# A four-layer conditioned transformer on one core: values by twos, layer 3's activations, negated minima, tables on GpSimd, lent score banks

## The chip, the core and the metric

The kernel runs on one core of a Trainium2 chip. Five engines work beside each other, each through a queue of its own in program order: TensorE (PE in the profile, its weight loads PEld), VectorE (DVE), ScalarE (ACT), GpSimd (POOL) and SyncE (SP), which issues most of the transfers. The metric is the time of one execution on the device in microseconds; less is better.

## The reference

Four layers follow each other on x of shape (4, 512, 512). All arithmetic is in float32. Every layer is conditioned on a vector of 512 per batch element. Cut to what matters:

```python
def layer0(x, t_emb, ...):            # 16 query heads of 32, 4 key heads, a window of 64 and every 64th token
    h = layernorm(x) * (1 + scale) + shift
    q = rope(h @ Wq.T); c = h @ Wkd.T; k = rope(c @ Wku.T); v = c @ Wvu.T
    attn = softmax(where(mask, -inf, q @ k.T / sqrt(32)))
    return x + (attn @ v) @ Wo.T

def layer1(x, pos, t, ...):           # 8 query heads of 64, 1 key head; then a gated MLP of 2048
    h = rms(x) * (w1 * (1 + t @ tw1.T))
    q = rope(h @ Wq.T, pos); k = rope(h @ Wk.T, pos); v = h @ Wv.T
    x = x + (softmax(q @ k.T / 8) @ v) @ Wo.T
    h = rms(x) * (w2 * (1 + t @ tw2.T))
    return x + (silu(h @ Wg.T) * (h @ Wu.T)) @ Wd.T

def layer2(x, cond, bias, ...):       # 16 heads of 32, normalised q and k; then an MLP of 2048
    h = ln(x) * (scale1 + 1) + shift1
    q, k, v = h @ Wqkv.T + [q_bias, 0, v_bias]
    q = q / max(norm(q), 1e-12) * sm; k = k / max(norm(k), 1e-12)
    x = x + (softmax(q @ k.T + bias) @ v @ Wproj.T + bproj) * gamma1
    h = gelu_tanh((ln(x) * (scale2 + 1) + shift2) @ Wfc1.T + bfc1)
    return x + (h @ Wfc2.T + bfc2) * gamma2

def layer3(x, emb, ...):              # 8 experts on 64 channels each, 64 -> 256 -> 64
    h = gelu(einsum('btel,elf->btef', x, W1) + b1)
    y = einsum('btef,efl->btel', h, W2) + b2
    hn = layernorm(y, g, b) * (1 + scale) + shift
    return x + silu(hn) @ out_W + out_b
```

## The kernel before

Tokens stand on the 128 partitions in four tiles of 128 (NT = 4), channels in four chunks of 128 (NC = 4). A weight unit of 512x512 (1 MB) is loaded as one transfer; rings of such units are loaded ahead.

Two streams run beside each other on TensorE and are woven by a planner. Stream A does the attention of layers 0 and 1 (stage a01) and of layer 2 (a2) for one batch element, stream M the MLPs: layer 1's (m1), layer 2's with layer 3 (m2). At the start there is no MLP yet, so M does batch 0's a01 while A does batch 1's. At the end A does batch 3's layer 2 MLP and the second half of its tokens in layer 3 (half1), M the first half (half0). A third strand, `conditioning`, computes the scales and shifts of all layers from ten weight units that pass one buffer (`late`) in turn.

Each stage is a Python generator that records operations and yields what it waits for. `Clocks` keeps a planned time for each engine and tile, with costs for each operation (`length`, `matmul`); `interleave` takes the next step from the stream whose inputs are ready and that is furthest behind its place. `evict` copies a bank from PSUM on ACT or DVE, whichever the plan has free sooner. At the end all operations are emitted in the order of their planned starts, so each engine's order is fixed in the built program. Because the calls go through one recorder, most rows of the profile have one line: L301 for DVE, ACT and POOL, L354 for matrix products, L360 for transposes, and the rows are told apart by their tiles.

PSUM has three pools of two: `two` (psS), tiles of two banks that take scores, and the banks of side A (psA) and side M (psM). `Side.bank` hands out a bank of its own side, `Side.at` says when one is free. Tile names: two = scores; probs and wm = probabilities of side A and M; pT and hid = transposed probabilities of side A and M (hid also hidden units); t and mt = work tiles; nq and mn = normed tokens or turned queries; h and mT = turned activations; late = the conditioning's unit, layer 1's table scratch, and later the bias of layer 2.

One attention unit is four heads (or two pairs) of one tile of 128 queries. `scores` makes products into two `two` tiles, takes the row maximum (`maxima`, or a plain reduction in layer 1), negates it in an own small operation (tile neg), and `soften` does the exponential with a sum on ACT, the reciprocal on DVE and the normalisation on POOL. `back` turns the probabilities by transposes through a side bank, and `values` multiplies them with v. `attention` runs them as a pipeline: the scores of unit i+1 go ahead of unit i's turning, and values follow two units behind, one unit at a time: a group of products into one bank and one eviction of 128 queries per unit.

Layer 2's attention first makes q, k, v by token tile: four tiles of q2, four of k2 (`product`), then four of v2; each q or k tile is copied by DVE, squared on ACT, reduced on DVE, raised to -1/2 on POOL (tile inv), multiplied on POOL, and turned (`heads_T`) one product later.

Layer 3 (`experts`): `first` takes for a pair of experts and each half f two banks, adds the bias to one on DVE and to the other on ACT, and then takes the Gelu over the whole hid tile in place; `second` and `third` make and turn y. Then `norm` (statistics on whole rows of 512, `norm_steps`), `turned` with gain and lift, a Silu over all four chunks, and the output's products.

Layer 1's rope tables (`tables`, `trig`: sine and cosine with an exact reduction of the angle) are computed on DVE for all positions at once (128x512), when batch 0's attention of layer 0 is about to begin; the conditioning waits for them, as they use its buffer.

Of the kernel before, what the change touches and what calls it, by code (L numbers as in the profile page):

```python
# [12 lines left out]
F32 = mybir.dt.float32  # L13
# [11 lines left out]
LOWEST = -3.0e38  # L25
# [283 lines left out]
def cond_seq_kernel(ctx: ExitStack, tc: tile.TileContext, a: dict, out: bass.AP):  # L309
# [89 lines left out]

    class Side:  # L400
# [8 lines left out]
        def bank(self):  # L409
            return clocks.tile(self.row_tag + "bank", 2, self.pools[0], (P, 512), "bank", name("bank"))  # L410

        def at(self, k=1):

            return clocks.free(self.row_tag + "bank", 2, k)
# [12 lines left out]
    class AttentionSide(Side):  # L427
# [28 lines left out]
        def pair(self):  # L456
            t = two_banks()
            return [t[:, 0, :], t[:, 1, :]]

        def pair_at(self):  # L460
            return clocks.free("two", 2)

    class OtherSide(Side):
# [25 lines left out]

        def pair(self):  # L490
            return [self.bank(), self.bank()]

        def pair_at(self):
            return self.at(2)
# [72 lines left out]
    def trig(ang, k, e, sin, nsin, cos):  # L567


        r = ang  # L570

        def nearest(period):
            vector.tensor_scalar(k, r, 1.0 / period, MAGIC, ALU.mult, ALU.add)
            vector.tensor_scalar(k, k, -MAGIC, None, ALU.add)

        def less(part):
            vector.scalar_tensor_tensor(r, k, -part, r, ALU.mult, ALU.add)

        far = TWO_PI * 2.0**17
        big = split(far, 2.0**8, 12, 2)  # L580
        nearest(far)
        less(big[0])
        less(big[1])
        vector.tensor_scalar(e, k, big[2], None, ALU.mult)
        nearest(TWO_PI)
        for part in split(TWO_PI, 2.0**-4, 7, 4):
            less(part)
        vector.tensor_tensor(r, r, e, ALU.subtract)
        nearest(TWO_PI)
        for part in split(TWO_PI, 2.0**-9, 12, 2):  # L590
            less(part)
        vector.tensor_scalar(r, r, PI_F32, -PI_F32, ALU.min, ALU.max)
        scalar.activation(e, r, AF.Abs)
        scalar.activation(sin, r, AF.Sin)
        scalar.activation(cos, e, AF.Sin, bias=half_pi, scale=-1.0)
        vector.tensor_scalar(nsin, sin, -1.0, None, ALU.mult)

    def tables(label, n, half, tokens, freqs):
# [3 lines left out]
        vector.tensor_tensor(  # L602
# [5 lines left out]
        parts = [const.tile([P, n * half], F32, name=f"{label}_{i}") for i in range(3)]  # L608
        trig(ang, k, e, *parts)
        return [t.rearrange("p (t i) -> p t i", i=half) for t in parts]  # L610
# [31 lines left out]
    def norm_steps(n, src, eps, rms=False, tiles=range(NT)):  # L642

        mv, own = tiny([P, NT, 2], "mv"), slice(tiles[0], tiles[-1] + 1)
        for t in tiles:
            st = tiny([P, 6], "st")
            vector.bn_stats(st, src[:, t, :])
# [83 lines left out]
    def maxima(p, s, bias, width, scale):  # L731

        mx = tiny([P, 2], "mx")
        for j in range(2):
            vector.tensor_tensor_reduce(
                out=p[:, j, 0:width], in0=s[:, j, 0:width], in1=bias, scale=scale, scalar=LOWEST,
                op0=ALU.add, op1=ALU.max, accum_out=mx[:, j : j + 1],
            )
        neg = tiny([P, 2], "neg")
        vector.tensor_scalar(neg, mx, -1.0, None, ALU.mult)  # L740
# [4 lines left out]
    def attention(side, units, scores, back, values, work, first, final=True):  # L745
# [15 lines left out]

        yield Until(scorable, of=first)
# [3 lines left out]
        for i, u in enumerate(units):  # L766
            cost, more = 0.0, i + 1 < len(units)
            when = [scorable] if more else []
            if len(late) == 2:
                yield Until(*when, side.at, of=late[0][1])  # L770
                values(*late.pop(0))
                cost += work[1]
            else:
                yield Until(*when)
# [9 lines left out]
        for u, pT in late:  # L784
            yield Until(side.at, of=pT)
            values(u, pT)
            yield work[1]
# [81 lines left out]
    coefs, tabs, ended = {}, {}, set()  # L869
# [16 lines left out]
    def attention0(b, side):  # L886
# [4 lines left out]
        if "0" not in tabs:  # L891
            tabs["0"] = tables("tab0", NT, 16, tok, freq[:, 32:48])
# [61 lines left out]
        def scores(u):  # L954
# [11 lines left out]
            for q, sc in zip(p, s):  # L966
                neg = maxima(q, sc, bias, n, 1.0 / math.sqrt(32.0))
                soften(q, q, neg, n, 1.0)
# [19 lines left out]
        def values(u, pT):  # L988
            c, qt = u
            (pT,), o, bl = pT, side.bank(), blocks(qt)  # L990
            for i, (at, n) in enumerate(bl):
                for g in range(4):
                    mm(
                        o[quarter(g), 0:P], lhsT=v[0:n, qt, i, quarter(g)],
                        rhs=pT[0:n, i, g * P : (g + 1) * P], start=i == 0, stop=i == len(bl) - 1,
                    )
            evict(ctxT[:, c, qt * P : (qt + 1) * P], o[:, 0:P])

        if "1" not in tabs:

            posf = const.tile([P, B * NT], F32, name="posf")
            vector.tensor_copy(posf, pos_i)
            tabs["1"] = tables("tab1", B * NT, 32, posf, freq[:, 0:32])
            ringC.load(1)
# [6 lines left out]
    def attention1(b, side):  # L1011
        n, wkv1 = side.n(), (yield from unit_for(b, "wkv1"))
        norm(n, xs[b], 1e-6, rms=True)
        yield from known("n1")
        hT = side.h()
# [66 lines left out]
        def values(u, pT):  # L1082
            c2, qt = u
            o = side.bank().rearrange("p (i q) -> p i q", q=P)
            for i in range(2):
                for at in range(NT):
                    for j in range(2):
                        mm(
                            o[half(j), i, :], lhsT=v[:, at, :], rhs=pT[i][:, j, at, :],
# [599 lines left out]
```

## Time and profile before

| | |
|---|---|
| median of 3 runs | 2498.31 us (2492.44 to 2498.45) |
| the profiled execution | 2497.25 us |
| its span, first to last instruction | 2495.5 us |
| mean granted TensorE clock | 0.992 |
| transposes of probs, 128x128 | 1600, 228.8 us busy |
| ACT table loads | 39, 50.0 us |
| DMA read | 147.83 MB, 61 GB/s with what is written |

A row of a group reads: line, engine, operation, out<-in, sizes, count | busy us and mean ns of one | the engine's idle time just before them and what ended most of it. A product in float32 leaves two records on TensorE, a transpose one. In a timeline the columns are start, length, engine, line, operation; the bracket is the engine's idle time before it and its releaser. Records of TensorE overlap, so the time that one takes from the engine is read from start to start.

### The profile page before, as it was taken

The numbers are of one execution on the slowest core, as the hardware profiler recorded it, in microseconds if no ns is written. First come the engines' busy times: TensorE is split into PE (matmuls) and PEld (weight loads), VectorE is DVE, ScalarE is ACT, GpSimd is POOL, SyncE is SP. The second block draws the span as 40 slices with busy tenths as digits, with TensorE's granted clock in tenths as the row PEclk, the third lists the DMA queues.
The fourth block names the chain that finished last, engine by engine and source line by source line (L and its number), as shares of the span: only waits on it lengthen the run. The fifth ranks groups of instructions, "written<-read, shape, count | busy, mean of one in ns | idle before, by whom it ended". The sixth has DMA issues, their size and how long they took to land.

```text
span 2495.5 us, 33420 instructions
## 1 busy us (share of the span) xinstructions
PE 2432.5 (97%) x12564; PEld 1242.0 (50%) x12564; DVE 1190.5 (48%) x3180; ACT 877.6 (35%) x2071; POOL 733.5 (29%) x921
## 2 busy tenths in 40 slices
PE   7989999999999999999999999999999999999997
PEld 4555655444554555554455455554455444554443
DVE  6766552133654454625554455443465333763233
ACT  2645441002551351414353043333255202651233
POOL 2433320005332223324222232424332205533221
PEclk9999999999999999999999999999999999999998
DMA  3220122220113111111211111112111221102210
GB/s 112 100 74 18 52 68 68 86 87 34 35 52 106 51 52 55 39 68 55 89 48 61 63 69 65 42 56 72 68 35 52 83 89 53 44 32 95 72 55 21
DMA packets 83312, 154.18 MB, mean 62 GB/s; under 512 B 3584, under 2 KB 10784, under 8 KB 83152
## 3 DMA queue, kind: packets, MB, share of 16 engines
q1 hardware_dynamic: 82544, 151.83, 17.9%
q8 instruction: 100, 1.64, 0.3%
q14 instruction: 60, 0.49, 0.1%
q0 software_dynamic: 176, 0.15, 0.1%
q10 hardware_dynamic: 432, 0.07, 0.0%
HBM read 147.83 MB, written 4.21 MB: 61 GB/s over the span
## 4 chain that ended last, share of the span: by engine, by line
PE 88%; DVE 3%; issue 3%; ACT 2%; POOL 2%; DMA 1%; ACTq 0%; POOLq 0%; DVEq 0%
PE bank L354 71%; PE bank L360 11%; PE two L354 6%; POOL inv L301 1%; ACT probs L301 1%; DVE probs L301 1%; ACT wm L301 0%; DVE neg L301 0%; POOL t L301 0%; DVE pT L301 0%; DMA late_ada_g<-in_units 0%; DMA wm<-in_units 0%; DVE t L301 0%; DMA late_ada_t<-in_units 0%; POOL probs L301 0%
## 5 line engine op out<-in xcount | busy, mean ns | idle before, releaser
L301 POOL TENSOR_SCALAR probs<-probs,inv 128x512 f32<-128x512 f32 (+4 forms) x544 | 316.4, 596 | 688.4 <-DVE inv L301 579.4
L301 ACT ACTIVATE probs<-probs,neg 128x512 f32<-128x512 f32 (+2 forms) x448 | 265.4, 594 | 254.8 <-DVE neg L301 254.3
L360 PEld LDWEIGHTS bank<-ident,probs 128*128 128x128 f32 (+2 forms) x1744 | 201.9, 141 | 161.9 <-issue 128.6
L360 PE MATMUL bank<-ident,probs 128*128 128x128 f32 (+2 forms) x1744 | 245.4, 276 | 4.1 <-ACT arow L301 1.2
L354 PE MATMUL bank<-mT,wm_gate 128*128 128x512 f32 x512 | 248.9, 597 | 0.0
L354 PE MATMUL bank<-mT,wm_up 128*128 128x512 f32 x512 | 245.7, 597 | 0.0
L354 PE MATMUL bank<-wm_down,hid 128*128 128x512 f32 x512 | 239.6, 596 | 0.7 <-DVE hid L301 0.7
L301 DVE CUSTOM_DVE_ANT_0 probs<-two,late 128x512 f32<-128x512 f32 x256 | 166.2, 686 | 74.3 <-PE two L354 56.4
L354 PE MATMUL bank<-wm_fc,hid 128*128 128x512 f32 x384 | 187.6, 594 | 0.0
L354 PE MATMUL bank<-mT,wm_fc 128*128 128x512 f32 x384 | 182.6, 597 | 0.0
L301 ACT COPY pT<-bank 128x512 f32<-128x512 f32 (+2 forms) x240 | 133.8, 580 | 83.8 <-PE bank L360 75.8
L354 PEld LDWEIGHTS bank<-pT,v 128*32 128x32 f32 (+2 forms) x3488 | 110.7, 116 | 95.9 <-issue 33.3
L354 PE MATMUL bank<-pT,v 128*32 128x128 f32 (+2 forms) x3488 | 146.0, 278 | 8.3 <-DVE pT L301 5.8
L301 ACT ACTIVATE mt<-bank 128x512 f32<-128x512 f32 x64 | 37.8, 591 | 327.6 <-PE bank L354 327.6
L354 PE MATMUL bank<-wa_q,h 128*128 128x512 f32 x320 | 152.4, 599 | 0.2 <-DVE t L301 0.2
L301 DVE TENSOR_TENSOR x<-x,bank 128x512 f32<-128x512 f32 x100 | 68.4, 684 | 176.1 <-PE bank L354 176.0
L354 PE MATMUL two<-kT,nq 32*128 32x512 f32 (+5 forms) x1088 | 150.0, 539 | 1.1 <-DVE mx L301 1.1
L354 PEld LDWEIGHTS bank<-wm_down,hid 128*128 128x128 f32 x512 | 91.7, 190 | 98.1 <-issue 96.2
L354 PEld LDWEIGHTS bank<-mT,wm_up 128*128 128x128 f32 x512 | 91.0, 190 | 98.2 <-issue 97.7
L301 DVE RECIPROCAL inv<-total 128x2 f32<-128x2 f32 x320 | 53.0, 166 | 172.9 <-ACT probs L301 155.7
L354 PEld LDWEIGHTS bank<-mT,wm_gate 128*128 128x128 f32 x512 | 90.0, 190 | 90.8 <-issue 90.3
L301 DVE COPY pT<-bank 128x512 f32<-128x512 f32 (+2 forms) x199 | 131.1, 680 | 5.9 <-PE bank L360 5.0
(221 smaller groups left out, 3396.3 us busy)
## 6 DMA issues: line engine op xcount, KB each, us to landing
wm_fc<-in_units SPq DMA_DIRECT2D x24, 1024.0 KB, 5.6
wm_gate<-in_units SPq DMA_DIRECT2D x16, 1024.0 KB, 5.7
wm_up<-in_units SPq DMA_DIRECT2D x16, 1024.0 KB, 5.7
wm_down<-in_units SPq DMA_DIRECT2D x16, 1024.0 KB, 5.4
wa_q<-in_units SPq DMA_DIRECT2D x10, 1024.0 KB, 5.5
wa_fc<-in_units SPq DMA_DIRECT2D x8, 1024.0 KB, 5.5
wa_o<-in_units SPq DMA_DIRECT2D x6, 1024.0 KB, 5.7
wa_k<-in_units SPq DMA_DIRECT2D x4, 1024.0 KB, 5.6
```

The source lines that it names most:

```text
L301: return call(*map(real, args), **{k: real(x) for k, x in kw.items()})
L354: latest[0] = nc.tensor.matmul(real(out), lhsT=real(lhsT), rhs=real(rhs), **kw)
L360: latest[0] = nc.tensor.transpose(real(out), real(src), unit)
```

## The change

The values of two units are taken together: `attention` waits until both are turned, and `values` gets both, fills one bank with 256 queries and evicts once. `maxima` becomes `lowest`: scores are scaled by the negative factor and the minimum is taken, which is the negated maximum, so the small negation goes; the exponential's scale is -1. (Layer 1's own reduction keeps its negation.) The mask or bias is added to the negated scores as it is.

Layer 1's tables are made by a generator of single operations on GpSimd, which `interleave` steps beside the streams (`chores`); a fused multiply-add becomes a multiply and an add there. Attention of layer 1 and the conditioning wait for them by name.

A `two` tile may be lent as a bank while no attention is between its first scores and its last values (`scoring`).

In layer 2 the products are ordered q2 x 4, k2 0, k2 1, then v2 0, k2 2, v2 1, k2 3, v2 2, v2 3; k is copied by `evict`, and the multiply with the inverse norm is on DVE.

In layer 3 the first products of a pair fill two `two` tiles (one for half the tokens), and the Gelu reads each bank with its bias; the statistics of y are taken per block of 128 as it is turned and aggregated; the Silu is h = z (1 + tanh z), with gain and lift halved beforehand: the tanh reads the bank on ACT, z and the product are made on DVE, per chunk.

```diff
@@ Side
         def bank(self):
+            if not scoring and clocks.now < self.own() > clocks.free("two", 2):
+                return two_banks()[:, 0, :]
             return clocks.tile(self.row_tag + "bank", 2, self.pools[0], (P, 512), "bank", name("bank"))
...
-        def at(self, k=1):
-            return clocks.free(self.row_tag + "bank", 2, k)
+        def own(self):
+            return clocks.free(self.row_tag + "bank", 2)
+        def at(self):
+            return self.own() if scoring else min(self.own(), clocks.free("two", 2))
@@ trig, tables (a generator now, on the engine given)
         def less(part):
-            vector.scalar_tensor_tensor(r, k, -part, r, ALU.mult, ALU.add)
+            if engine is vector:
+                vector.scalar_tensor_tensor(r, k, -part, r, ALU.mult, ALU.add)
+            else:
+                engine.tensor_scalar(sin, k, -part, 1.0, ALU.mult, ALU.mult)
+                yield Until(of=[sin])
+                engine.tensor_tensor(r, r, sin, ALU.add)
+            yield Until(of=[r])
@@ norm_steps
-            st = tiny([P, 6], "st")
-            vector.bn_stats(st, src[:, t, :])
+            if stats is None:
+                st = tiny([P, 6], "st")
+                vector.bn_stats(st, src[:, t, :])
+            else:
+                st = stats[:, t, :, :]
             vector.bn_aggr(mv[:, t, :], st)
@@ maxima -> lowest
-                out=p[:, j, 0:width], in0=s[:, j, 0:width], in1=bias, scale=scale, scalar=LOWEST,
-                op0=ALU.add, op1=ALU.max, accum_out=mx[:, j : j + 1],
+                out=p[:, j, 0:width], in0=s[:, j, 0:width], in1=bias, scale=-scale, scalar=HIGHEST,
+                op0=ALU.add, op1=ALU.min, accum_out=neg[:, j : j + 1],
             )
-        neg = tiny([P, 2], "neg")
-        vector.tensor_scalar(neg, mx, -1.0, None, ALU.mult)
         return neg
@@ attention
+        scoring.append(side)
         yield Until(scorable, of=first)
...
             if len(late) == 2:
-                yield Until(*when, side.at, of=late[0][1])
-                values(*late.pop(0))
-                cost += work[1]
+                yield Until(*when, side.at, of=late[0][1] + late[1][1])
+                values(late)
+                late = []
+                cost += 2 * work[1]
...
+        scoring.remove(side)
@@ attention0
         if "0" not in tabs:
-            tabs["0"] = tables("tab0", NT, 16, tok, freq[:, 32:48])
+            for _ in tables("0", NT, 16, tok, freq[:, 32:48], vector):
+                pass
+            posf = const.tile([P, B * NT], F32, name="posf")
+            vector.tensor_copy(posf, pos_i)
+            chores.append(tables("1", B * NT, 32, posf, freq[:, 0:32], gpsimd))
...
-        if "1" not in tabs:
-            posf = const.tile([P, B * NT], F32, name="posf")
-            vector.tensor_copy(posf, pos_i)
-            tabs["1"] = tables("tab1", B * NT, 32, posf, freq[:, 0:32])
-            ringC.load(1)
@@ values of attention2 (those of 0 and 1 in the same way)
-        def values(u, pT):
-            c, qt = u
-            o = side.bank()
-            for at in range(NT):
-                for g in range(4):
-                    mm(
-                        o[quarter(g), 0:P], lhsT=v[:, at, c * P + 32 * g : c * P + 32 * g + 32],
-                        rhs=pT[g // 2][:, g % 2, at, :], start=at == 0, stop=at == NT - 1,
-                    )
+        def values(two):
+            o, (c, first) = side.bank(), two[0][0]
+            for k, (_, pT) in enumerate(two):
+                for at in range(NT):
+                    for g in range(4):
+                        mm(
+                            o[quarter(g), k * P : (k + 1) * P],
+                            lhsT=v[:, at, c * P + 32 * g : c * P + 32 * g + 32],
+                            rhs=pT[g // 2][:, g % 2, at, :], start=at == 0, stop=at == NT - 1,
+                        )
@@ attention2
-        for which, dst in (("q2", qT), ("k2", kT)):
-            unit = side.ring.take(which)
-            for t in range(NT):
+        for which, t in [("q2", 0), ("q2", 1), ("q2", 2), ("q2", 3), ("k2", 0), ("k2", 1)] + [
+            x for i in range(2) for x in (("v2", i), ("k2", i + 2))
+        ] + [("v2", 2), ("v2", 3)]:
...
-                gpsimd.tensor_tensor(qv, qv, inv.unsqueeze(2).to_broadcast([P, 16, 32]), ALU.mult)
+                vector.tensor_tensor(qv, qv, inv.unsqueeze(2).to_broadcast([P, 16, 32]), ALU.mult)
@@ experts, first
+            yield Until(lambda: clocks.free("two", 2, 2 if n == S else 1), of=[xT[:, p, lo : lo + n], w1])
+            banks = [two_banks() for _ in range(2 if n == S else 1)]
...
-                    if j == 0:
-                        vector.tensor_scalar(at(j, f), s[j][:, 0:n], vec[:, bias : bias + 1], None, ALU.add)
-                    else:
-                        scalar.activation(at(j, f), s[j][:, 0:n], AF.Identity, bias=vec[:, bias : bias + 1])
-                yield 1.2 * n / S
-            for h in hid:
-                scalar.activation(h[:, :, 0:n], h[:, :, 0:n], AF.Gelu)
+                    scalar.activation(at(j, f), bank(j, f), AF.Gelu, bias=vec[:, bias : bias + 1])
@@ experts, third and after
+            for t in tiles:
+                vector.bn_stats(stats[:, t, p, :], y[:, t, p * P : (p + 1) * P])
...
-        norm(y, y, 1e-5, tiles=tiles)
+        norm(y, y, 1e-5, tiles=tiles, stats=stats)
         hT = side.late()
-        yield from turned(side, y, hT, b, coefs["gain"], coefs["lift"], tiles)
+        for c in range(NC):
+            yield Until(side.at, of=[y[:, t, c * P : (c + 1) * P] for t in tiles])
+            ps, h, z = side.bank()[:, 0:n], hT[:, c, own], side.t1()[:, 0:n]
+            for i, t in enumerate(tiles):
+                tr(ps[:, i * P : (i + 1) * P], y[:, t, c * P : (c + 1) * P], ident)
+            gain, lift = (coefs[x][:, c, b : b + 1] for x in ("gain", "lift"))
+            scalar.activation(h, ps, AF.Tanh, bias=lift, scale=gain)
+            vector.tensor_scalar(z, ps, gain, lift, ALU.mult, ALU.add)
+            vector.scalar_tensor_tensor(h, h, 1.0, z, ALU.add, ALU.mult)
-        scalar.activation(hT[:, :, lo : lo + n], hT[:, :, lo : lo + n], AF.Silu)
@@ interleave
+            while chores and chore_until.time <= clocks.now:
+                chore_until = next(chores[0], None)
```

## The prediction

> **What bounds the kernel.** I read the page's busy line and its chain of waits first: they say which engine sets the time.
>
> ```profile
> PE 2432.5 (97%) x12564; PEld 1242.0 (50%) x12564; DVE 1190.5 (48%) x3180; ACT 877.6 (35%) x2071; POOL 733.5 (29%) x921
> ...
> PE 88%; DVE 3%; issue 3%; ACT 2%; POOL 2%; DMA 1%; ACTq 0%; POOLq 0%; DVEq 0%
> ```
>
> TensorE is busy for 97% of the span and carries 88% of the chain, so only two things can shorten it: less TensorE time for the same products, or fewer of its idle 63 us (2495.5 - 2432.5). Busy time by stretches says where those lie (columns: length, PE busy, records, granted clock, DMA share, GB/s):
>
> ```profile
> 0.00:62.00 62.00, 47.65 (x224) 1.00 0.39 111
> 62.00:375.00 313.00, 289.30 (x2247) 0.97 0.18 62
> 375.00:1100.00 725.00, 723.21 (x3418) 1.00 0.18 62
> 1100.00:1180.00 80.00, 76.87 (x269) 1.00 0.17 56
> ...
> 1700.00:1780.00 80.00, 77.16 (x265) 0.98 0.16 56
> ...
> 2420.00:2496.00 76.00, 61.50 (x242) 0.88 0.06 21
> ```
>
> Idle: 14.4 at the start (9.3 of it before the first product, on the loads), 23.7 while both streams are in attention, 3.1 and 2.8 in two short stretches of layer 2, 14.5 at the end. Where an MLP runs beside attention (375 to 1100) it is 1.8 of 725: there only less TensorE time helps. The timeline of TensorE in that stretch shows what a product costs beyond its streaming:
>
> ```profile
> 881.99 2.74 PE L354 MATMUL bank<-wm_down,hid 128*128 128x512 f32 x6
> 884.66 0.65 PE L354 MATMUL bank<-pT,v 128*32 128x128 f32 x16
> 885.23 0.50 PE L354 MATMUL two<-kT,nq 32*128 32x128 f32 x8
> 885.67 1.09 PE L360 MATMUL bank<-ident,probs 128*128 128x128 f32 x8
> ```
>
> Count from start to start. Records of a full 128x128 product come 0.429 us apart, so six take 2.57; the values' products start after 2.67: leaving the full array costs 0.094. The 16 records of values, four side by side in 128x32 tiles, are 4 x 0.109 = 0.44 of streaming, and the scores start after 0.57: such a group carries 0.134 beyond its streaming. In the same way, from other rows of this timeline, a 64x128 group carries 0.204 (eight 512-wide records start to start 1.92, of which 1.72 streaming) and a 128x64 group 0.154.
>
> Two more rows of the groups:
>
> ```profile
> L360 PE MATMUL bank<-ident,t 128*128 128x128 f32 x244 | 38.2, 278 | 6.2 <-POOL t L301 6.0 <-DVE t L301 0.2
> L301 DVE TENSOR_SCALAR neg<-mx 128x2 f32<-128x2 f32 x320 | 67.7, 212 | 10.7
> ```
>
> **The change, part by part.**
>
> *Groups (values by twos, experts' two halves as one group).* The number of products is the same, 7,674. In the order in which TensorE's instructions stand, runs of equal array shape fall from 664 to 524: full array 258 to 208, 128x32 146 to 90, 128x64 64 to 48, 64x128 69 to 50, 32x128 127 to 128. Sum: 50 x 0.094 + 56 x 0.134 + 16 x 0.154 + 19 x 0.204 - 0.2 = 4.7 + 7.5 + 2.5 + 3.9 - 0.2 = 18.4. It comes off a busy TensorE, so it counts in full unless something else becomes late. I take -18, between -20 and -12 (a third of the groups lie before 375 us, where the softmax may set the pace). The 80 evictions of values that go save nothing: they run on DVE and ACT beside TensorE.
>
> *Layer 2's keys.* All 6.0 us that transposes of t waited for POOL lie here. One of them:
>
> ```profile
> 1761.71 2.90 POOL L301 TENSOR_TENSOR inv<-ss,neg_half 128x16 f32<-128x16 f32 x1 [6.97 <-DVE ss L301]
> 1764.69 1.05 POOL L301 TENSOR_TENSOR t<-t,inv 128x512 f32<-128x512 f32 x1
> 1765.78 0.42 PEld L360 LDWEIGHTS bank<-ident,t 128*128 128x128 f32 x4 [2.82 <-POOL t L301]
> 1765.79 0.66 PE L360 MATMUL bank<-ident,t 128*128 128x128 f32 x4 [1.99 <-POOL t L301]
> 1766.41 5.40 PE L354 MATMUL bank<-wa_v,h 128*128 128x512 f32 x8
> ```
>
> From a product's end to its transposes the tile needs copy, square, reduce, maximum, power (2.90), multiply: some 6.5 us. In the old order 4.3 us of TensorE work stand between the two in the worst two places and 5.8 in two more. The new order has 5.6 at least (two places) and 6.7 (two), as values' products stand among the keys'; and the multiply on DVE takes 0.69 (its 128x512 tensor-tensor row) for POOL's 1.05, so 6.1 are needed. Two half-microsecond waits stay: -5. The eight records after the wait took 5.2 us for 3.4, at a granted clock of 0.71: another -1.7 where the wait is gone. I take -6.5 (-2 to -8). The 32 multiplies add 22 us to DVE, which stood idle half of that time.
> The Trainium skill (TensorE: Matmul & The Clock Gate, Part 1) says that the clock halves after an idle window of about 3.4 us. This row shows it after a wait of 1.99 us, so by the page the 1.7 would not count and the sum would be 1.7 less; the row decides.
>
> *Start and the attention stretch.* DVE loses 21 operations on 128x512 for layer 1's tables between 24 and 60 us (its rows of late and tab: ten at 0.85, nine at 0.43, two at 0.69, together 13.8 us), which stood ahead of ropes and evictions; TensorE waited 0.84 twice there for a bank that a rope still read (now it borrows a score bank) and some 2 us more before the first scores. -3.5. POOL takes 19 tensor-scalars at 0.69 and 12 tensor-tensors at 1.27 (its rows of probs and of t on 128x512): 28 us. 19 of these 31 stand ahead of the first softmax unit, where POOL idled up to 14.3 us at a time; behind the other 12 stand the normalisations of 128x197 probabilities, and behind these the transposes: 12 x 0.69 to 1.27 is +8 to +15 if each were exposed, but POOL idled 1.5 to 2.6 before each normalisation, so +1.5. The tables' end moves the conditioning's ten loads back by some 20 us of TensorE work; its last product still stands 50 us ahead of the first MLP and far ahead of layer 2. The negation goes from 256 of 320 softmax pairs: 256 x 0.21 = 54 us of DVE, hidden where an MLP covers, 0.2 off the chain where none does: -2. Together -4 (-9 to +8).
> The Trainium skill speaks against the move (GPSIMD Engine Reference, section 4.1): elementwise work belongs on VectorE, as two-input operations are about twice as slow on GpSimd. The rows agree (1.27 for 0.69), and by the rule alone this part would cost its whole 28 - 14 = 14 us; it does so only if nothing covers it.
>
> *Layer 3.* The 80 bias additions of the experts, half on DVE and half on ACT, go; the Gelu reads PSUM with the bias (ACT 0.67 on 128x512, 0.47 on 256). The Silu becomes a tanh and two DVE operations a chunk, under a MLP for three batches. What counts is the end:
>
> ```profile
> 2474.40 0.71 POOL L301 TENSOR_TENSOR rstd<-var,neg_half 128x2 f32<-128x2 f32 x1 [20.11 <-DVE var L301]
> ...
> 2479.11 1.28 ACT L301 ACT_TABLE_LOAD   x1 [0.49 <-DVE h L301]
> 2480.40 1.06 ACT L301 ACTIVATE h<-h 128x1024 f32<-128x1024 f32 x1
> 2481.51 10.07 PE L354 MATMUL bank<-wm_out,h 128*128 128x512 f32 x16 [3.06 <-ACT h L301]
> ```
>
> Before: from the first turned chunk (2476.7) four transposes in turn, table load, Silu over all, then the product: 4.8 us. After: table load 1.28, tanh of one chunk 0.56, DVE 0.54, hops 0.2, and the product starts on it: 2.6. -2.2. Statistics by blocks spare the last tiles 0.8 (two of 0.69 become two on a quarter, bounded by 0.17 and 0.69). The 16 records took 10.07 instead of 6.9 at half clock: I count 1.0 of that. Against it: the eight products of the first half that covered the second half's Gelus stand ahead of them now, while ACT needs 4 x 0.47 a pair for 2.1 of TensorE: 0 (-3 to +4). I take -4 (-8 to +2).
>
> *New waits.* The values' products now take the newest unit's pT too, and the experts borrow both score tiles. By the order, the shortest cover of values goes from 1.8 to 1.1 us beside a need of about 1 (0.12 and an eviction of 0.56 to 0.69); experts get their tiles back after 2.9 to 3.4 us, with 0.25 + 2 x 0.67 + 1.28 (table load) = 2.9 needed. +2 (0 to +9).
>
> Sum: -18 - 6.5 - 4 - 4 + 2 = -30.5, against the profiled run's 2497.25 (1.75 above its span): 2466.8. The median shown is 1.1 above that run: 2468.
>
> **Rivals.** (1) The pace passes to the softmax: in 62 to 375 both streams are attention, and a third of the groups' 18 turn into waits; POOL's tables delay as well. For it: 23.7 idle there already. Against: 0.2 less chain and 14 us less DVE. -30.5 + 6 + 8 = -16: 2482. (2) Slower: the two score tiles become the bottleneck of layer 3. Three batches and two halves make 20 groups of first products; if these and as many second ones each wait for a table load in ACT's queue, that is 40 x 1.28 = 51, less 30.5: +20.5, 2519; it decides from 0.8 us a group on. For it: all waits for ACT here pass one in-order queue that also serves exponentials. Against: layer 2's attention at that time is at its projections, whose squares and copies load no table, and the built program has 30 table loads for 39. (3) No change: waits eat the gain evenly: 2493 to 2503; nothing in the MLP stretches speaks for it, with 1.8 us idle in 725.
>
> **How the numbers follow.** Forecast 2468, its own range 2456 to 2478: 0.72. Rival 1: 0.16. Rival 2: 0.06. Rival 3: 0.06. All terms at their good ends give 2453, at their bad ends 2503; 2450 to 2486 leaves out two in ten. A change of 0.3% (7.5 us) is about what a measurement here can tell: faster 0.87 (forecast, rival 1 but for a sliver), same 0.06, slower 0.07.
>
> **What would show it.** Right: value groups of 32 records start to start 1.0 (128-wide, two units); idle of transposes of t on POOL or DVE under 2; 62 to 375 shorter with no more idle; last wait before the final 16 records under 2.5 us. Wrong: more than 10 us of idle before first or second products of experts; transposes of wm or probs waiting for POOL over 8 us before 120 us; idle in the MLP stretches above 10.

## The result and the profile after

The changed kernel takes 2476.72 us (median of 6 runs, 2469.69 to 2479.10); the kernel before, run beside it, 2494.90 (6 runs). The ratio is 0.9924, 95% interval 0.9906 to 0.9942: faster by 0.76%, about 18 us. The forecast was 2468, so some 9 us of the gain are missing, more than the spread explains. The profiled execution took 2479.07 us with a span of 2477.3, against a span of 2495.5 before.

The busy line and the chain of the page, after:

```profile
PE 2413.0 (97%) x12564; PEld 1254.1 (51%) x12564; DVE 1123.4 (45%) x2902; ACT 865.2 (35%) x2076; POOL 726.5 (29%) x920
...
PE 91%; DVE 4%; ACT 2%; issue 1%; DMA 1%; POOL 1%; SPq 0%; POOLq 0%; DVEq 0%; ACTq 0%
```

TensorE's busy time fell by 19.5 us, where the prediction took 18 off for the groups; the mean granted clock did not rise (0.991 for 0.992). Its idle time did not fall: 2477.3 - 2413.0 = 64.3 us, for 63.0 before. All that was to be gained in waits was given back somewhere. Busy time by stretches says where (length, PE busy, records, granted clock, DMA share, GB/s):

```profile
0.00:62.00 62.00, 48.54 (x240) 0.97 0.38 110
62.00:375.00 313.00, 299.67 (x2314) 0.98 0.18 63
375.00:1100.00 725.00, 722.00 (x3387) 1.00 0.18 63
1100.00:1180.00 80.00, 78.17 (x278) 1.00 0.16 53
1180.00:1196.00 16.00, 3.89 (x10) 0.68 0.59 216
1196.00:1700.00 504.00, 502.87 (x2768) 1.00 0.16 55
1700.00:1780.00 80.00, 78.17 (x278) 1.00 0.11 38
1780.00:2420.00 640.00, 633.57 (x3117) 1.00 0.19 66
2420.00:2478.00 58.00, 46.17 (x186) 0.90 0.07 23
```

The stretch 62 to 375 has 13.3 us of idle for 23.7, and the last stretch, from 2420 to the end, 11.1 for 14.0. But in the 16 us from 1180 on, where nothing stood out before, TensorE is idle for 12.1 us. That is batch 1's attention of layer 2, at its products of queries, keys and values. TensorE's timeline, then VectorE's, GpSimd's and SyncE's show one chain (start, length, engine, line, operation; in brackets the idle time before and its releaser):

```profile
1168.90 3.60 PE L354 MATMUL bank<-wa_k,h 128*128 128x512 f32 x8
...
1193.63 1.09 PE L360 MATMUL bank<-ident,t 128*128 128x128 f32 x4 [12.11 <-DVE t L301]
```

```profile
1170.42 0.69 DVE L301 TENSOR_TENSOR t<-t,inv 128x512 f32<-128x512 f32 x1 [3.02 <-POOL inv L301]
1187.49 0.69 DVE L301 BATCH_NORM_STATS2 st<-x 128x6 f32<-128x512 f32 x1 [16.38 <-DMA x<-in_x]
1188.22 0.18 DVE L301 BATCH_NORM_AGGREGATE mv<-st 128x2 f32<-128x6 f32 x1
1188.32 0.66 DVE L301 COPY kT<-bank 128x512 f32<-128x512 f32 x1
1188.89 0.68 DVE L301 TENSOR_REDUCE ss<-t 128x16 f32<-128x512 f32 x1
...
1192.79 0.69 DVE L301 TENSOR_TENSOR t<-t,inv 128x512 f32<-128x512 f32 x1 [3.01 <-POOL inv L301]
```

```profile
1153.18 1.26 POOL L301 TENSOR_TENSOR x<-x,mt 128x512 f32<-128x512 f32 x1 [9.10 <-DVE mt L301]
...
1163.49 1.26 POOL L301 TENSOR_TENSOR x<-x,mt 128x512 f32<-128x512 f32 x1 [2.18 <-DVE mt L301]
```

```profile
1172.53 0.37 SPq L367 DMA_DIRECT2D wa_proj<-in_units  x1
1172.99 2.55 SPq L301 DMA_DIRECT2D out<-x  x4
1181.94 0.39 SPq L367 DMA_DIRECT2D x<-in_x  x1
```

Read from the bottom. SyncE issues proj2's load only at 1172.53, since its buffer was k2's and k2's last product, eight records from 1168.90, now comes after two of v2's. The four stores of batch 0's output stand behind it, although their rows had been ready from 1154.4 to 1164.8 (ends of GpSimd's additions). Batch 3's x goes into batch 0's buffer and so has to wait until the stores have landed: issued 1181.94, landed near 1187.5. On VectorE the first statistics of that x stand at the head of the queue, for 16.38 us, and behind them the last key tile's copy, reduction and multiply. The key tile is not related to this x at all; it only stands in the same queue. Before, SyncE had the same order, but there k2 was done with before v2 began, proj2's load did not hold the stores, and the statistics waited 2.51 us where nothing urgent stood behind them:

```profile
1168.60 0.37 SPq L367 DMA_DIRECT2D wa_proj<-in_units  x1
1185.98 14.15 SPq L301 DMA_DIRECT2D out<-x  x4
1202.00 0.39 SPq L367 DMA_DIRECT2D x<-in_x  x1
```

```profile
1207.74 0.69 DVE L301 BATCH_NORM_STATS2 st<-x 128x6 f32<-128x512 f32 x1 [2.51 <-DMA x<-in_x]
```

The code tells why the planner let it happen: `take("v2")` asks for proj2's load, and the plan's start of that load looks at the products of k2 that are planned so far. In the new order two are still to come, so the load, the stores and x were planned earlier than they can run, and the statistics were put into a gap of VectorE at x's planned arrival.

### The profile page after: what moved, and what is told of

Same layout as the page of the kernel before. It is cut to its first block, busy times and chain, and to the rows that moved or that the text cites. A ratio compares the mean times of both kernels' runs of the same rounds, so it can differ in the third digit from the quotient of the medians.

```text
span 2477.3 us, 33249 instructions
## 1 busy us (share of the span) xinstructions
PE 2413.0 (97%) x12564; PEld 1254.1 (51%) x12564; DVE 1123.4 (45%) x2902; ACT 865.2 (35%) x2076; POOL 726.5 (29%) x920
## 4 chain that ended last, share of the span: by engine, by line
PE 91%; DVE 4%; ACT 2%; issue 1%; DMA 1%; POOL 1%; SPq 0%; POOLq 0%; DVEq 0%; ACTq 0%
PE bank L354 70%; PE bank L360 11%; PE two L354 10%; DVE probs L301 1%; ACT probs L301 1%; DVE pT L301 1%; PE two L360 0%; DVE nq L301 0%; ACT wm L301 0%; DVE mx L301 0%; DMA out<-x 0%; DMA wm<-in_units 0%; DMA x<-in_x 0%; POOL probs L301 0%; DVE mt L301 0%
## 5 line engine op out<-in xcount | busy, mean ns | idle before, releaser
L354 PE MATMUL bank<-wm_down,hid 128*128 128x512 f32 x496 | 232.5, 597 | 0.0
L301 ACT COPY pT<-bank 128x512 f32<-128x512 f32 (+2 forms) x259 | 145.7, 577 | 78.2 <-PE bank L360 69.9
L301 POOL TENSOR_TENSOR inv<-ss,neg_half 128x16 f32<-128x16 f32 x32 | 92.8, 2901 | 131.6 <-DVE ss L301 131.6
L354 PE MATMUL bank<-pT,v 128*32 128x128 f32 (+2 forms) x3488 | 130.8, 275 | 0.3 <-DVE coef_s L301 0.3
L354 PE MATMUL bank<-wa_q,h 128*128 128x512 f32 x272 | 129.9, 596 | 0.0
L301 POOL TENSOR_TENSOR rstd<-var,neg_half 128x4 f32<-128x4 f32 (+1 forms) x25 | 24.7, 992 | 356.8 <-DVE var L301 356.6
```

What stands on the lines that cost most here:

```text
L301: return call(*map(real, args), **{k: real(x) for k, x in kw.items()})
L354: latest[0] = nc.tensor.matmul(real(out), lhsT=real(lhsT), rhs=real(rhs), **kw)
```

## The experiments

The theory from here on: the missing gain is this one wait, and it comes from the queues of SyncE and VectorE ("the theory" below; from e5 on it is the prediction's price of the part). The rival: the key chain itself (with a power of 2.9 us on GpSimd) is too long for the new order. All runs were timed in five rounds beside the kernel before, whose median was 2495.2, 2495.4 and 2493.9 in the three sets.

### Four ways around the wait

**e1: the statistics later on VectorE.** Only the plan of one arrival is moved.

```diff
         load(xs[b], a["x"][b].rearrange("(t p) c -> p t c", p=P))
+        if b == 3:
+            clocks.mark(xs[b], clocks.queue + 2.0 + 24.0, True)
```

> Only where batch 3's first statistics stand in VectorE's order changes: behind the last key tile's chain instead of ahead of it (the loads and their order stay). Theory (VectorE stands 16.4 us at the head of its queue on x's load, and the key chain waits behind it): the 12.3 us wait of TensorE at 1181 goes, with 1.2 of half-clock records after it; 2476.7 becomes 2461 to 2466, about 0.9875 of before. Rival (the key chain itself, with its 2.9 us power on GpSimd, is too long for the new order): nothing in that chain changes, so 2474 to 2479 and the wait still there.

Measured: 2463.71 us (2459.75 to 2463.84), ratio 0.9867 [0.9854, 0.9881]. SyncE's order and lateness are as before the edit, x's load even goes at 1184.29, but the key chain no longer stands behind it:

```profile
1175.71 0.69 DVE L301 COPY kT<-bank 128x512 f32<-128x512 f32 x1 [1.85 <-PE bank L360]
1176.55 0.69 DVE L301 TENSOR_REDUCE ss<-t 128x16 f32<-128x512 f32 x1 [0.15 <-ACT t L301]
1177.27 0.17 DVE L301 TENSOR_SCALAR ss<-ss 128x16 f32<-128x16 f32 x1
1180.46 0.69 DVE L301 TENSOR_TENSOR t<-t,inv 128x512 f32<-128x512 f32 x1 [3.01 <-POOL inv L301]
```

The chain ends 12 us earlier in the trace and TensorE is busy for all of the 16 us from 1180 on. The time is 13.0 us shorter with nothing in the key chain changed: the rival falls.

**e2: the old order of products in layer 2**, all else as changed.

```diff
-        for which, t in [("q2", 0), ("q2", 1), ("q2", 2), ("q2", 3), ("k2", 0), ("k2", 1)] + [
-            x for i in range(2) for x in (("v2", i), ("k2", i + 2))
-        ] + [("v2", 2), ("v2", 3)]:
+        for which, t in [(w, t) for w in ("q2", "k2", "v2") for t in range(NT)]:
```

> Layer 2's products stand as before (queries, keys, values); everything else is the changed kernel, the multiply on VectorE too. Theory: the last key product comes earlier, so proj2's load does not hold the stores and x's load on SyncE; the 12.3 us wait goes, 2 to 5 us of waits of key transposes come back over four batches: 2463 to 2470. Rival (the key chain): the same gain, as the order is what it blames; this run tells whether the order is the cause, not which way it acts. If the wait stays: both fall.

Measured: 2460.42 (2459.43 to 2460.95), ratio 0.9858 [0.9844, 0.9871]. The wait is gone. What I had not expected: the waits of key transposes did not come back. This row of the table of TensorE's waits is the same in e1 and in e2 (total, times, longest):

```profile
PE bank L360 <- DVE t L301: 4.0, 3, 1.8
```

So values among the keys had earned nothing; it had only brought the wait. e2 is the base of the later runs.

**e3: proj2's load asked for behind k2's last product.** `take("v2")` loads nothing ahead; the load follows `by_token` of k2's tile 3.

```diff
-                weights[which] = side.ring.take(which)
+                weights[which] = side.ring.take(which, ahead=1 if which == "v2" else None)
...
+                if (which, t) == ("k2", 3):
+                    side.ring.load(side.ring.taken + side.ring.ahead - 1)
```

> proj2's load is asked for behind the last key product, so on SyncE it stands behind the four stores and x's load; VectorE's order keeps the statistics ahead of the key chain. Theory: stores go at 1154 to 1165 as their rows are ready, x's load follows at 1168 to 1172 and lands 10 to 13 us earlier than 1187.5, the wait shrinks from 12.3 to 0 to 2.5 us: 2462 to 2469. Rival (the key chain): 2474 to 2479.

Measured: 2461.38 (2459.67 to 2463.85), ratio 0.9863 [0.9849, 0.9876]. SyncE's timeline:

```profile
1152.36 10.64 SPq L301 DMA_DIRECT2D out<-x  x4
1164.80 0.39 SPq L367 DMA_DIRECT2D x<-in_x  x1
1170.41 0.39 SPq L367 DMA_DIRECT2D wa_proj<-in_units  x1
```

The stores go as their rows are ready, x goes 17 us earlier than in the changed kernel, and the statistics, still ahead of the key tile, wait 1.34 us. By the trace, TensorE, VectorE, ScalarE and GpSimd have the changed kernel's order from the first instruction to the last; only SyncE's differs. With the new order of products and without its side effect the time is e2's, within the spread.

**e4: the stores on GpSimd's queue.** The diff is one word, `sync.dma_start(out=out...)` to `gpsimd.dma_start`. The order on TensorE, VectorE and ScalarE is that of the changed kernel.

> The out stores are issued by GpSimd's queue, each right behind the addition that it stores; TensorE, VectorE and ScalarE have the same order as the changed kernel. Theory: the stores leave SyncE, x's load goes right behind proj2's at 1173 instead of 1182, lands near 1179 to 1181, and the wait shrinks from 12.3 to 3 to 6 us: 2467 to 2472, if issuing stores costs GpSimd nothing that others wait for. Rival (the key chain): 2474 to 2480.

Measured: 2475.2 (2470.62 to 2476.56), ratio 0.9915 [0.9902, 0.9929]: a smaller gain than expected, with an interval that overlaps the changed kernel's. SyncE and TensorE:

```profile
1175.70 0.37 SPq L367 DMA_DIRECT2D wa_proj<-in_units  x1
1176.28 0.37 SPq L367 DMA_DIRECT2D x<-in_x  x1
1176.99 0.37 SPq L367 DMA_DIRECT2D wm_gate<-in_units  x1
```

```profile
1190.41 1.09 PE L360 MATMUL bank<-ident,t 128*128 128x128 f32 x4 [5.72 <-DVE t L301]
```

x's load now goes 0.58 us behind proj2's instead of 9.41, and the wait halves, as the theory says. It does not shrink further because x took 8.0 us from its issue to the start of its statistics at 1184.27, for 5.5 in the changed kernel. In both, three loads of 1 MB were issued within 1.3 us; in the changed kernel x was the first of them, here it is the second, behind proj2. That the place among them makes the difference fits, but no run tests it. The Trainium skill (DMA: Bandwidth & Descriptors, Issuing engines are not separate DMA queues) says that another issuer saves only the sequencer's time, as all transfers share the same 16 engines. The 8.0 us agree with the sharing; but what the other issuer saved here was the place in SyncE's queue, where the stores stood behind a load that waited for a buffer. The two profiled executions lie 5.2 us apart (2473.87 for 2479.07), not far from the 6.4 that the wait lost; the medians lie only 1.5 apart. So e4 shows which way the cause acts, and not its size.

### One part undone at a time

From e2, each part of the change is taken back alone. Their edits are the lines of the change reversed, so only what is taken back is told. A difference is that of the medians. e2 is of the first set, and the kernel before was 1.3 us faster in the third set (e10 to e13) than in the first, so a difference from e2 there is uncertain by about that much.

**e5: values one unit at a time**, with one eviction a unit.

> Base is e2_keys_first (2460.4). Values' products one unit at a time again (128 columns, one eviction a unit); the experts' merged halves stay. Runs of equal array shape on TensorE go from 524 to 617: 59 more of 128x32, 16 of 128x64, 19 of the full array: 59 x 0.134 + 16 x 0.154 + 19 x 0.094 = 12.2. Theory of the prediction (a group's price counts in full on a busy TensorE): +12, 2470 to 2475. Rival (in 62 to 375 us the softmax sets the pace, so the third of the groups there costs nothing, and the shorter chain of a single unit wins waits back): +5 to +8, 2465 to 2469.

2474.50 (2470.43 to 2478.28), ratio 0.9915 [0.9902, 0.9929]: +14.1, the theory.

**e6: layer 3's end with the Silu over all chunks, statistics on whole rows, gain and lift not halved.**

> Base is e2_keys_first (2460.4). Layer 3's end as before: statistics over whole rows, Silu over all chunks behind the four transposes; the experts' merged products stay. Theory of the prediction: 2.2 + 0.8 + 1.0 come back at the end, +4, 2463 to 2466, with a wait near 3 us before the final 16 records. Rival (what the end gains is given back ahead of it, in the experts' waits on two score tiles and one ACT queue, whatever the end looks like): +4 all the same at the end but nothing before it; so if the time rises by less than 2, the end's chain is not what the changed end saves.

2464.30 (2462.75 to 2466.13), ratio 0.9879 [0.9865, 0.9892]: +3.9. The wait before the final 16 records is 3.1 us again (for 0.83). The theory.

**e7: the experts' first products by pairs of banks, bias apart from the Gelu.**

> Base is e2_keys_first (2460.4). The experts' first products by pairs of banks again, the bias added apart from Gelu; the tanh end and the statistics by blocks stay. Theory of the prediction: 18 more groups of 64x128 and 16 of the full array, 18 x 0.204 + 16 x 0.094 = 5.2, all in layer 3: +3 to +6, 2463 to 2467. Rival (the lost cover at the end, priced 0 with bounds -3 to +4: eight products in a row stand ahead of the second half's Gelus): the pairs win back 2 to 4 us of waits between 2408 and 2460, so 0 to +2: 2459 to 2463.

2466.79 (2466.27 to 2469.82), ratio 0.9891 [0.9877, 0.9904]: +6.4, at the theory's upper end. The rival (0 to +2) falls: the lost cover at the end is not what counts.

**e9: layer 1's tables on VectorE**, ahead of the first softmax units.

> Base is e2_keys_first (2460.4). Layer 1's tables on VectorE again, where before had them, ahead of the first softmax units. Theory of the prediction (tables off VectorE are worth 3.5, on GpSimd they cost 1.5): +1 to +4, 2461 to 2465, lost between 25 and 120 us. Rival (GpSimd's 28 us of elementwise work delay the first normalisations and the conditioning's loads): faster, 2450 to 2459. By the trace the end of the conditioning and of the first stage moved by -10.6 to -16.9 between before and changed, which values' groups alone don't make: a second rival puts most of that down to the tables, +6 to +10.

2462.76 (2461.22 to 2466.53), ratio 0.9874 [0.9861, 0.9888]: +2.3, the theory's size, within the spread. The two rivals fall.

**e10: maxima and their negation** (layers 0 and 2).

> Base is e2_keys_first (2460.4). Layers 0 and 2 take maxima again and negate them in one more VectorE instruction a pair (256 x 0.21 = 54 us of VectorE). Theory of the prediction: 0.2 more on the chain of a softmax where no MLP covers it, +2 (0 to +4): 2460 to 2464. Rival (VectorE's in-order queue carries it everywhere): +6 to +10, 2466 to 2470.

2474.43 (2469.29 to 2477.78), ratio 0.9919 [0.9906, 0.9932]: +14.0, more than both. It is not spread out, as the rival had it: the first product of the first MLP (gate0) starts 13.6 us later than in e2 (355.6 for 342.0), and at the end of the span the distance is 14.9. Busy time from 62 to 375 us is 291.69 in e10, for 299.97 in e2. That stretch has layer 0's attention for two batches: 2 x 16 units x 2 pairs = 64 negations, at 0.21 us each 13.4 us. The size would fit a negation that stands on the chain in full, every time, but the trace does not bear this out: of the 13.6 us up to gate0's first product 8.4 are idle time of TensorE and 5.2 are busy time (from 100 to 140 us the granted clock is 0.83, for 0.91 in e2), and the conditioning's products also stand at other places. That the loss comes with the negations is measured; how they make it is open.

**e11: no lending of score banks** (`bank` and `at` know a side's own two alone).

> Base is e2_keys_first (2460.4). No score bank is lent: single banks come from each side's own two alone; the experts keep both score tiles. Theory of the prediction: 0.84 twice and part of 2 us before the first scores come back, +1 to +4: 2461 to 2464. Rival (lending moves waits about and spares none): -2 to +0.5, 2458 to 2461.

2473.76 (2471.23 to 2478.26), ratio 0.9923 [0.9910, 0.9936]: +13.3; both are wrong. By the trace the loss comes in steps: 3.1 before 342 us (no more than executions of one order differ by there, see the last section), about 2.4 between 540 and 700, 2.2 and 3.2 in layer 2's projections of batches 1 and 2, and some 3 at the end. Those two steps lie where layer 3's normed rows are turned beside the keys:

```profile
1139.10 1.04 PE L360 MATMUL bank<-ident,mn 128*128 128x128 f32 x8
1141.42 0.66 PE L360 MATMUL bank<-ident,mn 128*128 128x128 f32 x4 [1.28 <-ACT hid L301]
1143.06 0.66 PE L360 MATMUL bank<-ident,mn 128*128 128x128 f32 x4 [0.98 <-ACT hid L301]
```

In e2 the third and fourth of these groups go into a `two` tile with no wait. The new end holds a bank for the tanh and for VectorE's multiply, so it should need more banks in flight than the old one; this reason is argued, and no run tests it apart.

**e12: layer 2's multiply on GpSimd again** (order of products as before).

> Base is e2_keys_first (2460.4). The multiply of layer 2's queries and keys is on GpSimd again, 1.05 us for 0.69, behind the power in the same queue; the order is before's. In e2 the waits of key transposes are 4.4 us, no more than in the changed order, so of this part the multiply must have earned all: waits 6 to 8 us again, with half-clock records after them, +2 to +5: 2462 to 2466. Rival (neither order nor multiply earned anything, the saving came from the rest): 2459.5 to 2461.5.

2468.78 (2466.04 to 2474.26), ratio 0.9903 [0.9890, 0.9916]: +8.4, above the theory's range. The table of waits has, for 4.4 us in e2 on both engines together:

```profile
PE bank L360 <- POOL t L301: 8.1, 5, 3.0
```

and after the longest, the clock:

```profile
1136.83 1.11 PE L360 MATMUL bank<-ident,t 128*128 128x128 f32 x4 [3.00 <-POOL t L301]
1137.73 6.18 PE L354 MATMUL bank<-wa_k,h 128*128 128x512 f32 x8
```

Eight records of 3.60 us take 6.18. One would look for a queue on GpSimd, where multiply and power now both stand; at this wait it does not show:

```profile
1132.44 2.90 POOL L301 TENSOR_TENSOR inv<-ss,neg_half 128x16 f32<-128x16 f32 x1 [17.27 <-DVE ss L301]
1135.72 1.05 POOL L301 TENSOR_TENSOR t<-t,inv 128x512 f32<-128x512 f32 x1 [0.38 <-DVE inv L301]
```

GpSimd had been idle for 17.27 us when this tile's power came. The tile's own chain, from its addition on VectorE at 1130.10 to the end of the multiply at 1136.77, is longer than the one product of 3.60 us that TensorE has beside it. The second long wait, at 1733.61, looks the same (3.00, GpSimd idle for 17.28 before). In e2 the planner wove the streams differently here, and this tile's transposes did not wait at all. So the 8.4 us belong to the multiply with all that the plan does about it; a queue of powers and multiplies is not shown.

**e13: transposes two products behind**, tiles in the ring of pT.

```diff
-                q, sq = side.t1(), side.t2()
+                q, sq = side.some(), side.t2()
...
-                if late:
-                    yield from heads_T(side, *late)
-                late = (dst, t, q)
+                if len(late) == 2:
+                    yield from heads_T(side, *late.pop(0))
+                late.append((dst, t, q))
```

> Base is e2_keys_first (2460.4). A version meant to beat it: in layer 2 a tile's transposes stand two products behind its own product instead of one (the tiles lie in the ring of pT, which is free there). Theory: the two waits of 1.8 us at 1136 and 1731, where the key tile's reduction stands behind layer 3's rows on VectorE, go with the half-clock records after them: -3 to -6, 2454 to 2457.5. Rival (TensorE waits for something else right there, the rows of layer 3 or a bank): 2459 to 2462.

2457.67 (2452.99 to 2460.56), ratio 0.9852 [0.9838, 0.9866]: the fastest here, 1.5% below before. The waits of key transposes go from 4.4 to 0.7 us, and the span from 2457.6 to 2455.0. The medians differ by 2.8 us, at the theory's weak end, but by the ratios to the kernel before, each in its own set, e2 and e13 are only 1.5 us apart (0.9858 and 0.9852), and the intervals overlap. The waits are gone; a gain in time over e2 is not shown.

## Why the prediction was right, and where not

The direction and the main term were right, and the range just held: 2476.72 lies 1.3 us inside its end at 2478, and three of the six runs lie above it. The gain was 12 us smaller in the profiled executions (-18.2 for -30.5). The step that failed is **new waits**, "+2 (0 to +9)": it measured 13.0 (e1). I had looked for what now waits for a unit's pT and for the score tiles, and had checked the new order of layer 2 only for the transposes' cover. That order also moves the release of k2's weight buffer, so a load on SyncE, so everything behind it there. The sign that I had named fired: more than 10 us of idle in an MLP stretch. One sign of being right missed for the same reason: the transposes of t waited 16.5 us, for the "under 2"; in e1 they wait 4.4. Without this wait the prediction says -32.5, and e1's span is 33.7 below before's.

The other terms, with what each part costs when it is undone alone from e2:

| term of the prediction | said | undone alone |
|---|---|---|
| groups: values by twos | 12.2 of -18 | +14.1 |
| groups: experts' halves | 5.2 of -18 | +6.4 |
| layer 2's keys: the multiply | -6.5 with the order | +8.4 |
| layer 2's keys: the order | -6.5 with the multiply | -1.0 (e3 to e2) |
| tables on GpSimd | -2 (3.5 - 1.5) | +2.3 |
| negation | -2 | +14.0 |
| lent banks | within 3.5 | +13.3 |
| layer 3's end | -4 | +3.9 |

The last column adds up to 61.4 us, while e2 is only 34.8 below before: the parts are not independent. A wait that one part mends may partly be mended by another as well; and each run is planned anew, so an edit also moves what it does not name. Which of the two it is, the runs do not tell.

*Groups.* Right, mechanism and size. A pair's 32 records start at 888.82 and the next group at 889.84: 1.02 for the 1.0 named. That the softmax swallowed the early third of the groups has e5's total against it, 14.1 us where the full price is 12.2 and two thirds of it 8. (By gate0's first product e5 had lost 3.6 us, but executions of one order differ by more than that there.)

*Layer 2's keys.* The term was near in size and wrong in its reason. I put it down to cover from the new order (5.6 us) and 0.36 from the multiply. The order is worth nothing (e2 beside e3), the multiply 8.4, by a way that e12 does not show. The cover sum was off too: in e2 the two waits of 1.8 us come because layer 3's four rows stand on VectorE ahead of the key tile's reduction. After such a wait the clock stayed whole:

```profile
1731.48 0.66 PE L360 MATMUL bank<-ident,t 128*128 128x128 f32 x4 [1.83 <-DVE t L301]
1731.98 3.60 PE L354 MATMUL bank<-wa_k,h 128*128 128x512 f32 x8
```

Before, the wait of 1.99 us that the prediction shows was followed by eight such records in 5.40 us. The other wait of 1.99 us in the same execution was not:

```profile
1167.91 0.65 PE L360 MATMUL bank<-ident,t 128*128 128x128 f32 x4 [1.99 <-POOL t L301]
1168.53 3.70 PE L354 MATMUL bank<-wa_v,h 128*128 128x512 f32 x8
```

In e12, after two waits of 3.00 us, such records took 6.18 and 4.76. So the length of the wait alone does not say whether, or for how long, the clock halves. The Trainium skill's idle window of about 3.4 us (TensorE: Matmul & The Clock Gate, Part 1) is longer than all these waits, and three of them have half-clock records behind them.

*Start and attention stretch.* -4 was too small. By gate0 the changed kernel is 17 us ahead (342.3 for 359.3), where the prediction has 4 of this term and some 6 of the groups. The tables term held (2.3 for 2). The Trainium skill's rule (GPSIMD Engine Reference, section 4.1), that elementwise work belongs on VectorE, would have made e9 faster, and it is not; the multiply of e12 goes the rule's way. The tables stand beside the chain that TensorE waits for, the multiply stands on it. The negation I had priced at 2, "0.2 off the chain where none covers"; put back, it costs 14.0, nearly all before gate0, and why it is so much is open.

*Layer 3, the end.* Right in sum (3.9 for 4); the idle time in the last stretch before is 14.0 and not 14.5, as the span ends at 2495.5. From the first turned chunk, where the tanh starts, to the products it is 2.1 us, for 2.6 said and 4.8 before; no table load stands in it:

```profile
2461.23 0.56 ACT L301 ACTIVATE h<-bank,coef_lift,coef_gain 128x256 f32<-128x256 f32 x1 [3.41 <-PE bank L360]
...
2463.30 10.08 PE L354 MATMUL bank<-wm_out,h 128*128 128x512 f32 x16 [0.83 <-DVE h L301]
```

The half-clock part (1.0) did not come here: the 16 records still take 10.08. In e2 they take 8.98 and in e13 8.76, after the same wait of 0.83, and in e6, with the old end and a wait of 3.06, 8.84. So it does not belong to this term.

*Rivals.* The time measured lies nearer to the first rival's 2482 than to 2468, but not for its reason: the softmax did not take over the pace (idle from 62 to 375 fell), and GpSimd's tables delayed nothing that counts (transposes of probs waited 0.3 us for GpSimd in all). The score tiles did not become layer 3's bottleneck: products into them waited 3.1 us for hid in three places.

That the forecast came within 9 us owes something to errors that cancelled: undone alone, negation and lending are worth more than I said, while the order of the keys is worth nothing and brought the new wait.

## What to carry to other kernels

When products are reordered, follow each weight buffer to its release, the load that waits for it, and everything that stands behind that load in the issuing queue; then ask what stands at the head of each in-order compute queue for data from there. A wait that costs 2.5 us in one place costs 12 where an unrelated short chain stands behind it. A tiny operation cannot be priced by its share of a half-idle engine: putting back negations of 0.2 us cost 14. And before a single wait is explained by a queue, look whether the engine was idle just before.

## What the hardware showed that I had not expected

Beside what is told above of the clock (two waits of 1.99 us in one execution, eight records after them in 5.40 and 3.70) and of transfers side by side: one program can be some 5 us apart from itself at a place that no edit has touched. The changed kernel, e1, e3 and e4 have the same order on TensorE, VectorE, ScalarE and GpSimd up to gate0's first product, and the profiled executions start it at 342.3, 345.1, 340.2 and 345.5. Landmarks of two single executions are no better than that there.
